# A scan kernel with its skip term and B's turn as TensorE transposes, half of dt*x on VectorE, and a new order of issue

## The chip, the cores and the metric

The kernel runs on one core of a Trainium2 chip. A core has five engines that run their own instruction streams in order: TensorE (PE, matmuls and transposes; its weight loads are shown apart as PEld), VectorE (DVE), ScalarE (ACT), GpSimd (POOL) and SyncE (SP), which here only issues DMAs. They wait for each other by semaphores. Data lies in SBUF; PE writes its results to PSUM.

The metric is the time of one execution on the device in microseconds, from which the median of several runs is taken.

## The reference

The input is 16 images of 64 x 64 tokens with 128 channels. Layer 0 is a two-dimensional recurrent network and stays as it is. Layer 1 is a Mamba block that runs over the 4096 tokens of an image forwards and backwards, with the sum of both added to the input. Cut to what matters:

```python
dbl = xc @ x_w.T
dt, Bm, Cm = jnp.split(dbl, [DT_RANK, DT_RANK + D_STATE], axis=-1)
dt = jax.nn.softplus(dt @ dt_w.T + dt_b)
dA = jnp.exp(dt[..., None] * A)
dBx = dt[..., None] * Bm[:, :, None, :] * xc[..., None]
def step(h, inp):
    dA_t, dBx_t, C_t = inp
    h = dA_t * h + dBx_t
    y = jnp.einsum('bds,bs->bd', h, C_t)
    return (h, y)
...
y = jnp.swapaxes(ys, 0, 1) + xc * D
y = y * jax.nn.silu(z)
return y @ out_w.T
```

There are 256 inner channels (two halves of 128, called h = 0 and 1 below) and 16 states for each channel. All is in float32. D holds 256 factors, one for each channel.

## The kernel before

Layer 0 runs first (`layer0`). Layer 1 (`layer1`) then goes through 256 passes: for each of the 16 images 8 chunks of 512 tokens forwards and the same 8 backwards. A pass has the channels on the 128 partitions and the 512 tokens along the free dimension, once for each half.

In a pass, `conv` (PE) makes the convolved input, `silu` (ScalarE) makes `xc` of it, `xproj` (PE) and `xproj_take` (ScalarE) make `dbl`, which holds dt's low rank, B and C, tokens along the free dimension, in two blocks of 64 partitions for the two halves of the chunk. `dtproj` (PE) and `softplus` (ScalarE) make `dt`. `times` makes `dtx` = dt * xc, for both halves on GpSimd (line 1235). `decay` (ScalarE, line 1254) makes exp(dt * A) for each of the 16 states, and `scan` (VectorE, line 1308) runs the recurrence for each state and half: 32 scans of 512 tokens in a pass.

What goes into the scans besides the decays comes in two ways. For states 0 to 3, `drive` (GpSimd, line 1262) multiplies `dtx` by rows of B that a DMA has spread over all partitions; there the decay lies in a PSUM bank and the product in SBUF. For states 4 to 15, `drive_rows` (PE, line 1288) multiplies the turned `dtx` by a matrix `d` with B's values on diagonals; there the decay lies in SBUF and the product (`hps`) in PSUM. For `d`, `bturn` turns `dbl` on PE so that tokens lie on partitions (line 1182), `bturn_take` copies 12 of its columns to `bt` (ScalarE, line 1193), and `scatter` (SP, line 1271) writes `bt` to the diagonals of a matrix in DRAM, from which `spread` loads it (line 1207). `turn` and `turn_take` turn `dtx` itself.

The results are gathered in one PSUM bank `py` for each half, one half after the other. It begins with `skip` (PE): the matmul of `xc` with `ddiag`, a diagonal matrix of D that is built once, so that D * xc comes out turned, tokens on partitions. Then come `sums` (PE, transposes of `hc` that add up in PSUM, where `hc` is the scans' result times C by GpSimd's `out_of`, line 1331), and for the first four states `turned`, `turned_take` and `weigh`. Both `skip` and `sums` go through the helper `add`, so they share line 1368 and are told apart by their tiles (`py<-ddiag,xc` and `py<-ident,hc`). `finish` takes the half out of `py`; in the backward passes `again` adds the forward result, and `gate`, `back` and `project` lead to the output.

The order of the work on all engines is planned when the program is built: `order_of_issue` lists every operation with its engine, what it must follow and which buffers it takes, and `simulate` runs this list through a model with a cost for each operation (`COST`, `ISSUE`, `LINK`). An engine that is free takes the ready operation with the lowest urgency, and urgencies stand in the table `URGENCY`, one number for each operation in a forward and in a backward pass. The order in which the model begins the operations is the order in which they are issued. `RINGS` gives the number of buffers for each kind of tile, `AHEAD` by how much decays into PSUM banks may leave their order among themselves. The model only sets the order; on the chip each engine waits for what it needs.

Of the kernel before, what the change touches and what calls it, by code (L numbers as in the profile page):

```python
# [8 lines left out]
F32 = mybir.dt.float32  # L9
# [5 lines left out]
P = 128  # L15
# [29 lines left out]
def units_of(order):  # L45

    count = {}
    for x in order:
# [4 lines left out]
        else:  # L53
# [6 lines left out]
    "br": 2, "cr": 6, "bt": 2, "xc": 5, "dt": 4, "dtx": 3, "dtxt": 3, "dbl": 2, "z": 1, "y": 1,  # L60
# [5 lines left out]
    "bturn": 0.5, "bturn_take": 0.23, "xproj": 1.0, "xproj_take": 0.4, "times": 1.2,  # L66
    "turn": 0.47, "turn_take": 0.555, "decay": 0.68, "drive": 2.4, "drive_rows": 1.13,
    "scan": 1.21, "keep": 0.6, "keep_group": 0.57, "out": 2.39, "sums": 0.88, "skip": 0.89,
# [3 lines left out]
    "read_take": 0.56, "read_stats": 0.69, "normal": 3.0, "normalise": 0.75, "spread": 0.6, "rows": 0.81,  # L72
# [10 lines left out]
AHEAD = 3  # L83
# [3 lines left out]
ISSUE = {"b": 0.7, "c": 0.7, "d": 0.51, "k": 0.45, "scatter_d": 0.82, "scatter_k": 1.77}  # L87
# [3 lines left out]
        {(0, 0): 226.07, (0, 1): 225.5, (0, 2): 209.71, (0, 3): 245.13, (1, 0): -224.93, (1, 1): -215.88,  # L91
         (1, 2): -217.49, (1, 3): -219.71},
        {(0, 0): 240.75, (0, 1): 97.67, (0, 2): 239.83, (0, 3): 183.31, (1, 0): -224.93, (1, 1): -236.77,
         (1, 2): -236.93, (1, 3): -239.63},
    ),
    "xproj": (
        {(): -4.49},
        {(): 88.92},
    ),
    "xproj_take": (  # L100
        {(): 12.43},
        {(): -21.38},
    ),
    "rows": (
        {(): -45.24},
        {(): -121.72},
    ),
    "bturn": (
        {(): 244.05},
        {(): -26.43},  # L110
    ),
    "bturn_take": (
        {(): 158.86},
        {(): 159.8},
    ),
    "dtproj": (
        {(0,): -250, (1,): -53.81},
        {(0,): 50.32, (1,): 50.35},
    ),
    "times": (  # L120
        {(0,): -65.05, (1,): -67.57},
        {(0,): 244.56, (1,): -165.67},
    ),
    "turn": (
        {(0,): 249.76, (1,): -134.89},
        {(0,): 229.21, (1,): 221.57},
    ),
    "turn_take": (
        {(0,): 47.45, (1,): 47.51},
        {(0,): 227.25, (1,): 226.2},  # L130
    ),
    "skip": (
        {(0,): 103.25, (1,): 218.48},
        {(0,): 89.87, (1,): 208.37},
    ),
    "spread": (
        {("b", 0): 48.09, ("d", 0): 223.16, ("c", 0): 189.13, ("c", 1): 239.27, ("d", 1): -105.98, ("c",
         2): 8.58, ("c", 3): 235.49, ("b", 1): 201.1, ("d", 2): 56.35, ("c", 4): 230.23, ("c", 5):
         215.44, ("k", 0): 139.69},
        {("b", 0): -14.32, ("d", 0): 47.86, ("c", 0): -35.94, ("c", 1): 138.92, ("d", 1): -107.61, ("c",  # L140
         2): -218.83, ("c", 3): -181.78, ("b", 1): -3.62, ("d", 2): 122.62, ("c", 4): 54.73, ("c", 5):
         240.7, ("k", 0): 139.45},
    ),
    "drive": (
        {(0, 0): -56.91, (1, 0): -57.77, (0, 1): 215.02, (1, 1): 247.85},
        {(0, 0): 171.33, (1, 0): 123.34, (0, 1): 160.79, (1, 1): 118.53},
    ),
    "decay": (
        {(0, 0): 224.88, (4, 0): 226.48, (5, 0): 240.06, (6, 0): 188.37, (7, 0): 250, (1, 0): 113.5, (8,
         0): 247.75, (9, 0): 250, (10, 0): 249.7, (11, 0): 249.33, (2, 0): 123.95, (12, 0): 249.4, (13,  # L150
         0): 176, (14, 0): 177.57, (15, 0): 243.29, (3, 0): 220.69, (4, 1): 238.79, (5, 1): 203.28, (6,
         1): 109.72, (7, 1): 15.19, (0, 1): 44.93, (8, 1): 223.62, (9, 1): 223.58, (10, 1): 225.51, (11,
         1): 223.77, (1, 1): 148.26, (12, 1): 223.35, (13, 1): 66.54, (14, 1): 65.52, (15, 1): 156.31,
         (2, 1): 205.76, (3, 1): 245.25},
        {(0, 0): 114.51, (4, 0): 225.16, (5, 0): 225.14, (6, 0): 226.99, (7, 0): 226.82, (1, 0): 116.2,
         (8, 0): 248.06, (9, 0): -17.84, (10, 0): -182.05, (11, 0): 70.11, (2, 0): 180.88, (12, 0):
         152.1, (13, 0): 166.91, (14, 0): 113.63, (15, 0): 222.06, (3, 0): 31.92, (4, 1): 221.8, (5, 1):
         236.29, (6, 1): 241.63, (7, 1): 222.65, (0, 1): 243.59, (8, 1): 198.45, (9, 1): 228.52, (10, 1):
         31.86, (11, 1): 26.36, (1, 1): 192.12, (12, 1): 244.33, (13, 1): 245.68, (14, 1): 241.41, (15,
         1): 243.62, (2, 1): 241.76, (3, 1): 250},  # L160
    ),
    "scan": (
        {(0, 0): -110.99, (4, 0): -110.09, (5, 0): -105.1, (6, 0): -105.34, (7, 0): -105.61, (1, 0):
         181.32, (8, 0): 19.6, (9, 0): 19.21, (10, 0): -80.71, (11, 0): 7.49, (2, 0): 40.13, (12, 0):
         -108.17, (13, 0): -102.34, (14, 0): -10.85, (15, 0): -108.25, (3, 0): -48.47, (4, 1): -48.83,
         (5, 1): -68.91, (6, 1): -83.82, (7, 1): -96.92, (0, 1): -31.74, (8, 1): -33.58, (9, 1): -38.05,
         (10, 1): -40.96, (11, 1): -50.07, (1, 1): 200.94, (12, 1): -50.19, (13, 1): -87.76, (14, 1):
         -88.26, (15, 1): -91.09, (2, 1): -5.51, (3, 1): -86.39},
        {(0, 0): -109.51, (4, 0): -109.17, (5, 0): -109.22, (6, 0): 181.52, (7, 0): 181.62, (1, 0):
         181.29, (8, 0): 178.29, (9, 0): 89.91, (10, 0): 53.07, (11, 0): 78.05, (2, 0): 236.4, (12, 0):  # L170
         238.58, (13, 0): 235.96, (14, 0): 231.8, (15, 0): 185.76, (3, 0): 215.03, (4, 1): -224.25, (5,
         1): -76.4, (6, 1): -164.06, (7, 1): -249.08, (0, 1): -59.15, (8, 1): 43.77, (9, 1): 17.69, (10,
         1): -44.01, (11, 1): 39.93, (1, 1): 179.06, (12, 1): 225.25, (13, 1): 220.27, (14, 1): 219.29,
         (15, 1): 208.64, (2, 1): 205.77, (3, 1): -93.1},
    ),
    "scatter": (
        {("d", 0): -144.33, ("d", 1): 131.97, ("d", 2): -55.93, ("k", 0): 242},
        {("d", 0): 229.49, ("d", 1): 250, ("d", 2): -140.49, ("k", 0): 202.88},
    ),
    "drive_rows": (  # L180
        {(0, 0): 146.61, (1, 0): 105.78, (2, 0): 191.69, (0, 1): 31.86, (1, 1): 23.35, (2, 1): 216},
        {(0, 0): 117.29, (1, 0): -235.5, (2, 0): -209.5, (0, 1): -218.03, (1, 1): -1.36, (2, 1): 220.27},
    ),
    "keep": (
        {(0, 0): 243.5, (1, 0): 34.18, (2, 0): 129.78, (3, 0): -79.15, (4, 0): 159.92, (5, 0): -249.25,
         (0, 1): 66.3, (1, 1): 176.21, (2, 1): 144.92, (3, 1): -209.94, (4, 1): 140.89, (5, 1): 96.84},
        {(0, 0): -158.59, (1, 0): 220.66, (2, 0): 74.58, (3, 0): -133.66, (4, 0): 174.52, (5, 0): 249.16,
         (0, 1): -179.84, (1, 1): -6.05, (2, 1): -230.81, (3, 1): -175.76, (4, 1): -72.61, (5, 1): 0.64},
    ),
    "out_of": (  # L190
        {(0, 0): 108.7, (1, 0): -34.28, (2, 0): -83.46, (3, 0): 208.24, (4, 0): 161.27, (5, 0): -58.6,
         (0, 1): 206.6, (1, 1): -49.46, (2, 1): -49.85, (3, 1): -249.28, (4, 1): -201.46, (5, 1): 30.29},
        {(0, 0): 70.5, (1, 0): -63.47, (2, 0): -69.72, (3, 0): 41.7, (4, 0): 117.41, (5, 0): 29.34, (0,
         1): -114.11, (1, 1): -106.56, (2, 1): -250, (3, 1): -250, (4, 1): -242, (5, 1): -12.92},
    ),
    "sums": (
        {(0, 0): 211.83, (1, 0): 214.79, (2, 0): 204.06, (3, 0): -118.64, (4, 0): 34.31, (5, 0): -162.93,
         (0, 1): 232.47, (1, 1): 221.1, (2, 1): 203.91, (3, 1): 184.07, (4, 1): -222.45, (5, 1): -216.44},
        {(0, 0): -193.31, (1, 0): -194.97, (2, 0): -209.87, (3, 0): -189.32, (4, 0): -201.67, (5, 0):
         -91.54, (0, 1): 250, (1, 1): 236.49, (2, 1): 104.24, (3, 1): 225.82, (4, 1): 240.77, (5, 1):  # L200
         166.95},
    ),
    "keep_group": (
        {(0, 0): 208.79, (0, 1): -155.94},
        {(0, 0): -223.05, (0, 1): -200.24},
    ),
    "turned": (
        {(0, 0, 0): -242.59, (0, 0, 1): 198.86, (0, 0, 2): -19.69, (0, 0, 3): -164.84, (0, 1, 0): 211.89,
         (0, 1, 1): -221.33, (0, 1, 2): -221.83, (0, 1, 3): -131.66},
        {(0, 0, 0): -224.04, (0, 0, 1): 147.65, (0, 0, 2): -245.55, (0, 0, 3): -163.35, (0, 1, 0):  # L210
         142.63, (0, 1, 1): 126.52, (0, 1, 2): 128.31, (0, 1, 3): 130.7},
    ),
    "turned_take": (
        {(0, 0, 0): 63.6, (0, 0, 1): 44.72, (0, 0, 2): 65.41, (0, 0, 3): 65.32, (0, 1, 0): -184.53, (0,
         1, 1): 128.22, (0, 1, 2): 127.61, (0, 1, 3): 106.49},
        {(0, 0, 0): 55.23, (0, 0, 1): 9.13, (0, 0, 2): 192.65, (0, 0, 3): 192.3, (0, 1, 0): -181.41, (0,
         1, 1): -222.89, (0, 1, 2): 132.46, (0, 1, 3): 131.21},
    ),
    "weigh": (
        {(0, 0): -231.65, (0, 1): -206.75},  # L220
        {(0, 0): -4.68, (0, 1): 4.67},
    ),
# [1276 lines left out]
```

## Time and profile before

| | us |
|---|---|
| median of 3 runs | 12,566.69 (12,562.89 to 12,603.51) |
| profiled execution | 12,569.44 |
| its span, first to last instruction | 12,567.3 |

Busy time over the whole span, layer 0 with it:

| engine | busy us | share |
|---|---|---|
| PE | 12,114.5 | 96% |
| PE weight loads | 9,486.8 | 75% |
| VectorE | 11,138.3 | 89% |
| ScalarE | 9,954.8 | 79% |
| GpSimd | 10,578.2 | 84% |

The granted PE clock is 0.99 of full speed over the span, the DMA engines are busy a little over half of the time. Layer 0 takes the first 1,500 us or so, in which GpSimd has little to do; from there on the profile is even to the end. Matmuls are pipelined and their ends are modelled, so PE's busy time isn't its load. Rows of groups give the engine, the operation, the tiles written and read with their shape, the count, the busy time, the mean duration of one in ns, and the idle time of the engine just before them with what ended it.

### The profile page before, as it was taken

To read this page: it belongs to the slowest core of one execution; us is meant where nothing else is said; L and a number is where in the kernel's file an instruction comes from. 1 tells how busy PE (TensorE), PEld (TensorE's weight loads), DVE (VectorE), ACT (ScalarE), POOL (GpSimd) and SP (SyncE) were. 2 spreads that over 40 slices of the span, in tenths; PEclk is the share of its full clock that TensorE was granted. 3 is DMA by queue.
4 is the path that set the end of the run, shared out by engine and by line. 5 is a ranking of instruction groups with operands and counts; after the bars stand their busy time and mean duration, and the time that the engine had idled before them with its cause. 6 is when DMAs were issued, how large, how long until landed. Compare 5 with 4: busy or idle time off the path is not lost. (4 is left out here: it accounts for less than half of the span.)

```text
span 12567.3 us, 322625 instructions
## 1 busy us (share of the span) xinstructions
PE 12114.5 (96%) x128820; PEld 9486.8 (75%) x128820; DVE 11138.3 (89%) x11409; ACT 9954.8 (79%) x15936; POOL 10578.2 (84%) x4868
## 2 busy tenths in 40 slices
PE   9999999999999999999999999999999999999999
PEld 8656877777777777777777777777777777777777
DVE  7767699998989999999999998999999999999998
ACT  3444588888888888888888888888888888888887
POOL 0111299999999999999999999999999999999998
PEclk9999899999999999999999999999999999999999
DMA  4222255555556555555555555555555555556564
GB/s 156 56 56 56 64 162 160 158 166 158 160 157 166 159 160 158 165 160 158 167 159 162 158 163 161 162 163 158 162 158 163 159 163 161 162 159 165 158 164 140
DMA packets 2320782, 1885.92 MB, mean 150 GB/s; under 512 B 1537696, under 2 KB 1883312, under 8 KB 2319280
## 3 DMA queue, kind: packets, MB, share of 16 engines
q1 hardware_dynamic: 2241328, 1830.04, 52.2%
q10 hardware_dynamic: 77952, 35.24, 1.2%
q8 instruction: 1017, 16.66, 0.5%
q14 instruction: 485, 3.97, 0.1%
HBM read 1698.25 MB, written 164.30 MB: 148 GB/s over the span
## 5 line engine op out<-in xcount | busy, mean ns | idle before, releaser
L1331 POOL TENSOR_TENSOR hc<-hst,cr 128x1024 f32<-128x1024 f32 x3072 | 7384.9, 2431 | 465.0 <-DVE hst L1308 307.3
L1308 DVE TENSOR_TENSOR_SCAN hst<-da,carry,hps 128x512 f32<-128x512 f32 x5376 | 6466.2, 1261 | 535.0 <-issue 219.7
L1254 ACT ACTIVATE da<-dt,A_log_sb 128x512 f32<-128x512 f32 x8192 | 5404.7, 710 | 843.3 <-DVE hst L1308 783.9
L1368 PEld LDWEIGHTS py<-ident,hc 128*128 128x128 f32 x24576 | 2763.6, 142 | 769.0 <-issue 358.3
L1368 PE MATMUL py<-ident,hc 128*128 128x128 f32 x24576 | 3108.0, 275 | 165.7 <-POOL hc L1331 154.5
L1262 POOL TENSOR_TENSOR group<-dtx,br 128x1024 f32<-128x1024 f32 x1024 | 2447.0, 2403 | 134.8 <-PE ptg L1340 85.8
L1308 DVE TENSOR_TENSOR_SCAN group<-da,carry,group 128x512 f32<-128x512 f32 x1792 | 2243.8, 1266 | 118.9 <-ACT da L1254 108.3
L1288 PEld LDWEIGHTS hps<-d,dtxt 32*128 32x128 f32 x49152 | 1526.0, 187 | 621.8 <-issue 280.3
L1125 PE MATMUL pp<-xT,wk 128*128 128x512 f32 x4096 | 1954.8, 599 | 1.7 <-ACT dt L1229 1.2
L1288 PE MATMUL hps<-d,dtxt 32*128 32x128 f32 x49152 | 1810.0, 283 | 139.4 <-DVE hst L1308 117.3
L1348 ACT COPY ht<-ptg 128x512 f32<-128x512 f32 x2048 | 1126.9, 588 | 430.6 <-PE ptg L1340 398.9
L887 POOL TENSOR_TENSOR a_f<-a_f,c 128x16 f32<-128x16 f32 (+35 forms) x254 | 188.6, 743 | 1313.9 <-ACT a_f L879 1250.2
L1340 PE MATMUL ptg<-ident,group 128*128 128x128 f32 x8192 | 1153.0, 278 | 35.4 <-DVE group L1308 18.5
L1340 PEld LDWEIGHTS ptg<-ident,group 128*128 128x128 f32 x8192 | 922.4, 142 | 256.9 <-issue 91.9
L1125 PEld LDWEIGHTS pp<-xT,wk 128*128 128x128 f32 x4096 | 697.5, 190 | 524.9 <-issue 496.1
L1308 DVE TENSOR_TENSOR_SCAN hst<-da,hps 128x512 f32<-128x512 f32 x768 | 874.6, 1199 | 83.8 <-PE hps L1288 46.4
L1235 POOL TENSOR_TENSOR dtx<-dt,xc 128x512 f32<-128x512 f32 x512 | 646.8, 1288 | 61.6 <-DMA d<-d 29.5
L1254 ACT ACT_TABLE_LOAD x527 | 676.1, 1283 | 9.4
L1368 PE MATMUL py<-ddiag,xc 128*128 128x128 f32 x4096 | 580.2, 285 | 13.3 <-ACT y L1415 10.8
L1355 PE MATMUL py<-ht,k 128*32 128x128 f32 x16384 | 559.8, 277 | 2.6 <-ACT ht L1348 1.2
L879 ACT ACTIVATE a_f<-pg_f,b_sb 128x16 f32<-128x16 f32 (+35 forms) x508 | 219.7, 472 | 415.2 <-DMA x<-xl 212.7
L1368 PEld LDWEIGHTS py<-ddiag,xc 128*128 128x128 f32 x4096 | 496.2, 191 | 59.3 <-ACT y L1415 25.4
(113 smaller groups left out, 12431.2 us busy)
## 6 DMA issues: line engine op xcount, KB each, us to landing
cr<-rows SPq DMA_DIRECT2D x1536, 512.0 KB
d<-d SPq DMA_DIRECT2D x768, 448.0 KB
br<-rows SPq DMA_DIRECT2D x512, 512.0 KB
k<-k SPq DMA_DIRECT2D x256, 256.0 KB
yf<-y SPq DMA_DIRECT2D x128, 512.0 KB
yl<-yf SPq DMA_DIRECT2D x128, 512.0 KB
carry<-hst SPq DMA_DIRECT2D x3072, 1.0 KB
xs<-in_x_dram SPq DMA_DIRECT2D x64, 512.0 KB
```

What stands on the lines that cost most here:

```text
L879: nc.scalar.activation(agv.rearrange("p i b -> p (i b)"), pgv, AF.Tanh if g == "c" else AF.Sigmoid, bias=b_sb[:, gi : gi + 1],)
L1125: nc.tensor.matmul(self.ps["conv", h], lhsT=wk[:, k, h * P : (h + 1) * P], rhs=xT[self.b % 2][:, t0 : t0 + T], start=(k == 0), stop=(k == ...
L1235: nc.gpsimd.tensor_mul(self.dtx[h], self.dt[h], self.xc[h])
L1254: nc.scalar.activation(t, self.dt[h], AF.Exp, scale=amat[:, h, s : s + 1])
L1262: nc.gpsimd.tensor_mul(both[:, m : m + 2, :], bc(self.dtx[h], 1, 2), self.brow[q])
L1288: nc.tensor.matmul(part[:, j, :, :], lhsT=self.dtxt[h][rows, j, :], rhs=dg[rows, j + r, :, :], start=True, stop=True, skip_group_check=True,)
L1308: nc.vector.tensor_tensor_scan(t[:, self.rev], self.da.pop((s, h))[:, self.rev], dbx[:, self.rev], 0.0 if self.first else carry[:, self.d, ...
L1331: nc.gpsimd.tensor_mul(self.hc[g, h], self.hst[g, h].rearrange("p t m -> p m t"), self.crow[g])
L1340: nc.tensor.transpose(pt[:, k, :], self.group[g, h][:, t0 : t0 + TB, :].rearrange("p t s -> p (t s)"), ident,)
L1348: nc.scalar.copy(t, self.ps.pop(("turned", g, h, j)))
L1355: nc.tensor.matmul(self.py[h][q * TB : (q + 1) * TB, j * P : (j + 1) * P], lhsT=cd[:, GX * j + q, :], rhs=self.ht[g, h, j][:, q, :], start ...
L1368: nc.tensor.matmul(self.py[h][:, cols], **{"start": False, "stop": False, **how}, skip_group_check=True)
```

## The change

Five things change.

1. `skip` becomes a transpose. ScalarE first makes `xd` = xc * D in a new operation `scaled` (one for each half, ring of two buffers), and PE adds its four 128 x 128 blocks to `py` as transposes against the identity. `ddiag` goes.
2. `bturn` becomes four transposes of 128 rows in place of eight matmuls of 64 x 64. Its result lies on 64 partitions, with the two halves of the chunk side by side, so `bt` has 96 columns on 64 partitions instead of 48 on 128, and each `scatter` of a `d` becomes two DMAs of 64 partitions, six in a pass instead of three.
3. `times` of the second half runs on VectorE, that of the first stays on GpSimd.
4. `dtx` has two buffers instead of three, and `AHEAD` is 0 instead of 3.
5. Some costs of the planner are set anew, and all urgencies are.

```diff
-    "br": 2, "cr": 6, "bt": 2, "xc": 5, "dt": 4, "dtx": 3, "dtxt": 3, "dbl": 2, "z": 1, "y": 1,
+    "br": 2, "cr": 6, "bt": 2, "xc": 5, "xd": 2, "dt": 4, "dtx": 2, "dtxt": 3, "dbl": 2, "z": 1, "y": 1,
...
-    "bturn": 0.5, "bturn_take": 0.23, "xproj": 1.0, "xproj_take": 0.4, "times": 1.2,
-    "turn": 0.47, "turn_take": 0.555, "decay": 0.68, "drive": 2.4, "drive_rows": 1.13,
-    "scan": 1.21, "keep": 0.6, "keep_group": 0.57, "out": 2.39, "sums": 0.88, "skip": 0.89,
+    "bturn": 0.5, "bturn_take": 0.28, "xproj": 1.0, "xproj_take": 0.4, "times": 1.28, "times_dve": 0.62,
+    "turn": 0.47, "turn_take": 0.555, "decay": 0.68, "drive": 2.4, "drive_rows": 1.12,
+    "scan": 1.22, "keep": 0.62, "keep_group": 0.5, "out": 2.43, "sums": 0.92, "skip": 0.45, "scaled": 0.68,
...
-AHEAD = 3
+AHEAD = 0
...
-ISSUE = {"b": 0.7, "c": 0.7, "d": 0.51, "k": 0.45, "scatter_d": 0.82, "scatter_k": 1.77}
+ISSUE = {"b": 0.45, "c": 0.44, "d": 0.46, "k": 0.34, "scatter_d": 1.2, "scatter_k": 0.65}
...
-                put("times", (h,), "POOL", after=[("softplus", i, h), ("silu", i, h)],
-                    takes=[T_["dtx"][h]], uses=[T_["xc"][h], T_["dt"][h]], chain=("times", 0))
+                put("times", (h,), "DVE" if h else "POOL", C_["times_dve"] if h else None, after=[("softplus", i, h), ("silu", i, h)],
+                    takes=[T_["dtx"][h]], uses=[T_["xc"][h], T_["dt"][h]], chain=("times", h))
...
-            put("skip", (h,), "PE", after=[("silu", i, h)], takes=[py[h]], uses=[T_["xc"][h]], chain=("skip", 0))
+            xd = tile_of("xd")
+            put("scaled", (h,), "ACT", after=[("silu", i, h)], takes=[xd], uses=[T_["xc"][h]], chain=("scaled", 0))
+            put("skip", (h,), "PE", after=[get(("scaled", i, h))], takes=[py[h]], uses=[xd, T_["xc"][h]], chain=("skip", 0))
...
-                pt = self.ps["bturn"] = bank(place, f"pbt_{self.nm}", (P, NB, QP))
+                pt = self.ps["bturn"] = bank(place, f"pbt_{self.nm}", (QP, NB, P))
                 strided = self.dbl.rearrange("p (i j) -> p j i", j=NB)
                 for j in range(NB):
-                    for q in range(NQ):
-                        part = slice(q * QP, (q + 1) * QP)
-                        nc.tensor.matmul(
-                            pt[part, j, :],
-                            lhsT=strided[part, j, :],
-                            rhs=ident[part, part],
-                            start=True,
-                            stop=True,
-                            skip_group_check=True,
-                        )
+                    nc.tensor.transpose(pt[:, j, :], strided[:, j, :], ident)
...
-                self.bt = ring(cp, "bt", [P, NB, NS - NX], f"bt_{self.nm}")
-                nc.scalar.copy(self.bt, self.ps.pop("bturn")[:, :, RANK + NX : RANK + NS])
+                self.bt = ring(cp, "bt", [QP, NB, NQ, NS - NX], f"bt_{self.nm}")
+                pt = self.ps.pop("bturn").rearrange("p j (q s) -> p j q s", q=NQ)
+                nc.scalar.copy(self.bt, pt[:, :, :, RANK + NX : RANK + NS])
...
-                nc.gpsimd.tensor_mul(self.dtx[h], self.dt[h], self.xc[h])
+                (nc.vector if h else nc.gpsimd).tensor_mul(self.dtx[h], self.dt[h], self.xc[h])
...
-                    dst = bass.AP(t.tensor, t.offset, [[WD + GX, P], [P, NB], [1, GX]])
-                    nc.sync.dma_start(dst, self.bt[:, :, GX * g : GX * (g + 1)])
+                    for q in range(NQ):
+                        dst = bass.AP(
+                            t.tensor, t.offset + q * QP * (WD + GX), [[WD + GX, QP], [P, NB], [1, GX]]
+                        )
+                        nc.sync.dma_start(dst, self.bt[:, :, q, GX * g : GX * (g + 1)])
...
+            def scaled(self, h):
+                self.xd[h] = ring(cp, "xd", [P, T], f"xd_{self.nm}_{h}")
+                nc.scalar.activation(self.xd[h], self.xc[h], AF.Copy, scale=dvec[:, h, :])
+
             def skip(self, h):
 
                 for j in range(NB):
                     self.add(
                         h,
                         slice(j * P, (j + 1) * P),
-                        lhsT=self.xc[h][:, j * P : (j + 1) * P],
-                        rhs=ddiag[:, h, :],
+                        lhsT=self.xd[h][:, j * P : (j + 1) * P],
+                        rhs=ident,
+                        is_transpose=True,
                     )
```

## The prediction

> **What bounds it now.** I read the page's busy shares first, then a table of stretches, then the groups of instructions between 3000 and 12000 us, then the waits of VectorE, and last two timelines. The chain of waits is of no use here: the page follows it over a few steps and gives every share as 0%.
>
> The groups show 209 passes between 3000 and 12000 us (418 `times` instructions, two a pass). A pass so takes 9000 / 209 = 43.06 us, and the 256 passes of layer 1 take 11,023 us; the rest, some 1,540 us, is layer 0, where only the building of `ddiag` goes. All that follows is per pass, times 256.
>
> The stretch (columns: length, then busy us of PE, weight loads, VectorE, ScalarE, GpSimd):
>
> ```profile
> 3000.00:12000.00 9000.00, 8679.55 (x99538) 6864.47 (x99537) 8229.28 (x7147) 7587.61 (x11748) 8480.52 (x3762) 1.00 0.58 161
> ```
>
> Divided by 209: GpSimd 40.58 us, VectorE 39.37, ScalarE 36.30. PE's 41.5 is modelled and no measure. GpSimd bounds the loop, 2.48 us under the pass; VectorE has 3.69 us of idle time. Who ends VectorE's idle time:
>
> ```profile
> DVE hst L1308 <- issue: 193.4, 457, 1.5
> DVE group L1308 <- ACT da L1254: 124.6, 208, 1.8
> DVE hst L1308 <- PE hps L1288: 120.7, 196, 1.8
> DVE hst L1308 <- POOL hc L1331: 87.1, 142, 1.7
> DVE y L1417 <- PE py L1355: 69.0, 186, 0.7
> DVE hst L1308 <- POOL group L1262: 46.3, 61, 1.6
> ```
>
> No one wait carries it. Waits ended by PE (120.7 + 69.0 here, 23.1 in smaller rows) and by GpSimd (133.4 here, 10.9 for `dtx`) make 357 us, 1.71 a pass. The loop is balanced between three engines, so work taken from one counts only as far as the next allows.
>
> **Skip and B's turn on PE.** From the timeline at 6000 us (start, duration, count):
>
> ```profile
> 6004.83 0.75 PE L1242 MATMUL ptx<-ident,dtx 128*128 128x128 f32 x4
> ...
> 6005.60 1.16 PE L1368 MATMUL py<-ddiag,xc 128*128 128x128 f32 x8
> ...
> 6034.98 0.42 PEld L1340 LDWEIGHTS ptg<-ident,group 128*128 128x128 f32 x4
> 6034.99 0.65 PE L1340 MATMUL ptg<-ident,group 128*128 128x128 f32 x4
> ...
> 6044.65 1.17 PE L1182 MATMUL pbt<-ident,dbl 64*64 64x64 f32 x16
> ```
>
> An fp32 matmul counts as two instructions, a transpose as one: `skip` of one half is 8 now and 4 after. The row nearest to the new skip (four transposes of contiguous data) is ptg, 0.65 us: 1.16 - 0.65 = 0.51 saved, twice a pass, 1.02 us. The Trainium skill ("TensorE: Matmul & The Clock Gate", Terms) calls the transpose mode four times faster for fp32; by that, an estimate, skip would fall to 1.16 / 4 = 0.29 and save 1.74 us a pass. The rows give 1.16 / 0.65 = 1.8 times at this size, and I take them. `bturn`'s 16 instructions become 4 strided transposes, whose row is ptx: 1.17 - 0.75 = 0.42. PE sheds 1.44 us a pass. It doesn't set the end alone, so this pays only through VectorE's waits for PE and the sums' place behind them.
>
> The groups from which the next costs come (count, then busy us and mean ns of one; busy over count is the spacing):
>
> ```profile
> L1331 POOL TENSOR_TENSOR hc<-hst,cr 128x1024 f32<-128x1024 f32 x2508 | 6029.8, 2431 | 375.1 <-DVE hst L1308 242.4 <-DMA cr<-rows 61.0 <-issue 29.1
> ...
> L1254 ACT ACTIVATE da<-dt,A_log_sb 128x512 f32<-128x512 f32 x6695 | 4418.1, 710 | 690.4 <-DVE hst L1308 641.7 <-DVE group L1308 40.4
> ...
> L1348 ACT COPY ht<-ptg 128x512 f32<-128x512 f32 x1672 | 920.4, 588 | 336.3 <-PE ptg L1340 310.1
> ...
> L1235 POOL TENSOR_TENSOR dtx<-dt,xc 128x512 f32<-128x512 f32 x418 | 528.2, 1288 | 27.2 <-ACT dt L1229 18.5
> ```
>
> **ScalarE.** Two `scaled` of 128x512. Lowest by the plain copies of 128x512 (920.4 / 1672 = 0.55 us), highest by the normalise, also SBUF to SBUF (76.4 / 103 = 0.74), and I take the decay's row, which has a scale by partition and no bias (4418.1 / 6695 = 0.66): 1.32 us. No table load: copies stand between exponentials today without one. `bturn_take` moves 96 elements in place of 48, by the slope between the 256- and 512-wide copies (0.367 and 0.588 us) 0.04 more. ScalarE 37.66 us, hidden by its 6.8 us of idle time, because `xc` is ready two passes ahead. If that cover were gone, all 1.36 us would go to the decays behind, 348 us in the run.
>
> **SP.** Three more scatters, 0.50 us each by the median of `d<-bt`: 1.5 us on a queue that mostly waits for scans. Behind them stand `d`, `k`, the C rows and the carries. PE has no wait that ends with `d`'s landing; GpSimd waits for C rows 0.29 us a pass. I count nothing; with every such wait doubled, 75 us.
>
> **dt*x.** GpSimd loses 528.2 / 418 = 1.26 us. VectorE gains an instruction with two SBUF inputs, while its scans and products in layer 1 each have one data operand in PSUM. Layer 0 shows what that means, in the timeline at 802 us:
>
> ```profile
> 802.16 1.17 POOL L887 TENSOR_TENSOR a_f<-a_f,c 128x464 f32<-128x464 f32 x1 [7.40 <-ACT a_f L879]
> ...
> 802.65 1.18 DVE L888 TENSOR_TENSOR a_f<-a_f,c 128x464 f32<-128x464 f32 x1 [1.63 <-ACT a_f L879]
> ...
> 803.93 0.64 DVE L890 TENSOR_TENSOR a_f<-a_f,a_f 128x464 f32<-128x464 f32 x1
> ```
>
> The same shape takes 0.64 us with GpSimd idle (L890) and 1.18 beside it (L888). L888 ends 0.50 us after GpSimd's end (803.83 against 803.33), so it begins to stream only when GpSimd is through. In layer 1 GpSimd is busy 94% of the time, in pieces of 2.42 us (16 a pass) and 1.29. The mean rest of a running piece is (16 x 2.42² + 1.29²) / (2 x (16 x 2.42 + 1.29)) = 1.19 us, times 0.94 = 1.12 us. Then 512 elements at L888's rate after the release, 0.55 us. So `times` of the second half costs VectorE 1.67 us, not 0.69 (0.64 plus 48 elements), and the planner plans 0.62. No row shows the other direction. The Trainium skill ("SBUF — State Buffer", two separate sides) says that the pair of ports is locked for a whole instruction and the other engine blocks fully; by it GpSimd stands 0.55 us. By the row alone GpSimd falls to 39.32, with the rule to 39.87, 141 us in the run apart. I take the rule, since the row fits the lock exactly. What the page doesn't say is who comes first when a next GpSimd instruction is queued as well. Queued behind the waiting product are the scans, for which GpSimd, PE and ScalarE's decays wait.
>
> **Edits with one answer.** One `dtx` buffer fewer: `times` of a pass waits for the same half's drives of the pass before; at most it doubles the 0.22 us a pass in `hst <- POOL group`; I count nothing. `AHEAD` 0, the costs and the urgencies only reorder: what they bring can't be read from this profile, and it is the widest unknown. I bound it by the idle time, at best all 1.71 us that VectorE waits for PE and GpSimd, at worst none of it.
>
> **Sum.** VectorE 39.37 + 1.67 = 41.04 becomes the largest load. Of its idle 3.69 us, the waits for PE (less loaded by 1.44) and GpSimd (by 0.71) go in part: all gone gives 41.04 + 1.98 = 43.02 (10 us less in the run), half gone 43.88 (+210 us). I take three quarters, 1.28: 41.04 + 2.41 = 43.45, +0.39 x 256 = +100 us, nearer to the low end because both engines in front have new slack, and not at it because the issue order was laid out for a VectorE that doesn't wait. The profiled execution took 12,569.4 us (span 12,567.3); the median 12,566.7 is the same within 3 us. Forecast **12,667 us**, own range 12,605 to 12,780.
>
> **Rivals.**
> 1. *Faster: GpSimd goes on to decide.* VectorE's wait falls into its 3.69 us of idle time, and the pass follows GpSimd: 39.87 + 2.48 = 42.35, -0.71 x 256 = -182, **12,385 us**. For it: VectorE waits as often as GpSimd is busy, and GpSimd is largest today. Against: idle VectorE time is mostly there to wait for inputs, and the product doesn't bring them sooner. It decides as soon as over 1.3 us of the added 1.67 lie in old gaps. Were there no lock at all, 41.80 and 12,244.
> 2. *Slower by much: the product loses the race.* If GpSimd's queued instruction takes the ports first, the product waits one more piece, 2.42 us: 43.45 + 2.42 = 45.87, +719, **13,286 us**. For: GpSimd runs its pieces without gap. Against: a request that already waits should be served, and layer 0, with one piece at a time, can't tell.
> 3. *Nothing measurable:* relief and wait cancel, **12,567 us**, as the low end of the sum already has it.
>
> **Chances.** Forecast case 0.46, rival 1 0.33, rival 2 0.10, rival 3 0.11. A change under 0.3% (38 us) can't be told from none here. So faster 0.33, same 0.11, slower 0.56. The range for 8 in 10 goes from rival 1's number to well above the forecast case and leaves out most of rival 2 and rival 1's lower part: 12,400 to 12,940. For the forecast case alone it is 12,605 to 12,780.
>
> **What would show it.** Right: `dtx` on VectorE with a mean near 1.7 us and a spread from 0.7 to 3; some GpSimd instructions 0.5 us longer beside it; skip as 4 instructions in 0.65 us; VectorE's share up to 94 or 95%, GpSimd's down to 92%; two ACT instructions of 0.7 us a pass without new table loads; the granted clock still 1.00. Wrong: `dtx` at 0.7 us (no lock, then rival 1 or better), `dtx` over 3 us (rival 2), or waits of VectorE for `da` or `hps` that grow, which would put the loss on the order of issue and not on the ports.

## The result, and the profile after

| | before | after |
|---|---|---|
| median, us | 12,577.49 (12,562.89 to 12,603.51, 4 runs) | 13,051.31 (13,008.00 to 13,067.97, 4 runs) |
| profiled execution, its span | 12,569.44, 12,567.3 | 13,008.0, 13,006.2 |

The changed kernel is slower: ratio 1.0369, 95% interval 1.0336 to 1.0402. That is 474 us by the medians, and 439 us between the two profiled executions, from which all that follows is read.

The stretch from 3000 to 12000 us of the kernel after (columns as in the prediction: busy us of PE, weight loads, VectorE, ScalarE, GpSimd, then the granted clock, the DMA share and GB/s):

```profile
3000.00:12000.00 9000.00, 8165.16 (x91695) 6378.92 (x91693) 8238.95 (x7086) 7525.26 (x11717) 7992.38 (x3420) 0.98 0.55 155
```

It holds 201 passes, so a pass takes 9000 / 201 = 44.78 us, 1.72 more than before; times 256 that is 440 us, the whole difference of the profiled executions. Per pass (measured busy time, and idle time as the rest of the pass):

| us per pass | before | predicted | after |
|---|---|---|---|
| VectorE busy | 39.37 | 41.04 | 40.99 |
| GpSimd busy | 40.58 | 39.87 | 39.76 |
| ScalarE busy | 36.30 | 37.66 | 37.44 |
| VectorE idle | 3.69 | 2.41 | 3.79 |
| GpSimd idle | 2.48 | 3.58 | 5.02 |

The loads are as predicted within 0.3 us. The loss lies in idle time: VectorE's didn't shrink, and GpSimd's doubled. Groups of instructions of the kernel after in that stretch (count, busy us and mean ns of one, then idle time just before them and what ended it):

```profile
L1382 ACT ACTIVATE xd<-xc,D_sb 128x512 f32<-128x512 f32 x402 | 289.2, 719 | 60.5 <-PE py L1365 54.9
...
L1229 DVE TENSOR_TENSOR dtx<-dt,xc 128x512 f32<-128x512 f32 x201 | 385.9, 1920 | 0.0
...
L1328 POOL TENSOR_TENSOR hc<-hst,cr 128x1024 f32<-128x1024 f32 x2415 | 5827.6, 2437 | 564.3 <-DVE hst L1305 201.6 <-issue 132.0 <-PE ptg L1337 120.9
...
L1256 POOL TENSOR_TENSOR group<-dtx,br 128x1024 f32<-128x1024 f32 x804 | 1968.7, 2454 | 387.9 <-DMA carry<-group 172.6 <-PE ptg L1337 95.2 <-DVE group L1305 26.0
```

The last row is the one to stop at: GpSimd's products for states 0 to 3 (`drive`, four in a pass) now wait 387.9 us in this stretch, 172.6 of them by name for the DMA of `keep_group`, which copies the last column of a `group` tile into `carry` for the next chunk. The same group before:

```profile
L1262 POOL TENSOR_TENSOR group<-dtx,br 128x1024 f32<-128x1024 f32 x836 | 1998.0, 2404 | 117.3 <-PE ptg L1340 74.7 <-DMA carry<-group 20.9 <-DVE hst L1308 15.4
```

The two new transposes, in the timeline of the kernel after (start, duration, count):

```profile
6009.77 0.65 PE L1182 MATMUL pbt<-ident,dbl 128*64 128x128 f32 x4
...
6012.45 0.66 PE L1365 MATMUL py<-ident,xd 128*128 128x128 f32 x4
```

And who ends VectorE's waits, after (us in total, times, longest):

```profile
DVE hst L1305 <- POOL hc L1328: 240.2, 274, 3.5
...
DVE hst L1305 <- PE hps L1285: 140.6, 168, 2.7
...
DVE group L1305 <- ACT da L1248: 56.7, 56, 2.9
...
DVE y L1419 <- PE py L1352: 3.2, 13, 0.3
```

VectorE's wait for GpSimd's outputs rose from 87.1 to 240.2 us; its waits for the sums on PE fell from 69.0 to 3.2, and those for the decays from 124.6 to 56.7. Some waits went as hoped, and one took their place: VectorE stands for a GpSimd that itself came late.

### The profile page after: what moved, and what is told of

Same layout as the page of the kernel before. It is cut to its first block, busy times and chain, and to the rows that moved or that the text cites. A ratio compares the mean times of both kernels' runs of the same rounds, so it can differ in the third digit from the quotient of the medians.

```text
span 13006.2 us, 313375 instructions
## 1 busy us (share of the span) xinstructions
PE 11893.2 (91%) x123700; PEld 9220.6 (71%) x123700; DVE 11524.1 (89%) x11663; ACT 10233.8 (79%) x16448; POOL 10362.6 (80%) x4612
## 5 line engine op out<-in xcount | busy, mean ns | idle before, releaser
L1365 PE MATMUL py<-ident,hc 128*128 128x128 f32 x24576 | 3208.4, 279 | 350.7 <-POOL hc L1328 349.7
L1365 PEld LDWEIGHTS py<-ident,hc 128*128 128x128 f32 x24576 | 2817.0, 144 | 806.9 <-POOL hc L1328 522.2
L1256 POOL TENSOR_TENSOR group<-dtx,br 128x1024 f32<-128x1024 f32 x1024 | 2508.5, 2456 | 481.6 <-DMA carry<-group 236.5
L1127 PE MATMUL pp<-xT,wk 128*128 128x512 f32 x4096 | 1898.5, 600 | 0.5 <-DVE xl L913 0.5
L1337 PE MATMUL ptg<-ident,group 128*128 128x128 f32 x8192 | 1208.0, 280 | 113.6 <-DVE group L1305 45.6
L1127 PEld LDWEIGHTS pp<-xT,wk 128*128 128x128 f32 x4096 | 739.0, 193 | 711.3 <-issue 684.9
L1213 PE MATMUL pv<-dbl,dt_wT 128*128 128x256 f32 x2048 | 519.9, 383 | 0.0
L1352 PEld LDWEIGHTS py<-ht,k 128*32 128x32 f32 x16384 | 410.6, 110 | 133.1 <-issue 75.8
L1229 DVE TENSOR_TENSOR dtx<-dt,xc 128x512 f32<-128x512 f32 x256 | 467.5, 1826 | 3.8 <-ACT dt L1223 3.8
```

What stands on the lines that cost most here:

```text
L1127: nc.tensor.matmul(self.ps["conv", h], lhsT=wk[:, k, h * P : (h + 1) * P], rhs=xT[self.b % 2][:, t0 : t0 + T], start=(k == 0), stop=(k == ...
L1213: nc.tensor.matmul(pv[:, q * TQ : (q + 1) * TQ], lhsT=dt_wT[:, q, h * P : (h + 1) * P], rhs=self.dbl, start=True, stop=True,)
L1229: (nc.vector if h else nc.gpsimd).tensor_mul(self.dtx[h], self.dt[h], self.xc[h])
L1256: nc.gpsimd.tensor_mul(both[:, m : m + 2, :], bc(self.dtx[h], 1, 2), self.brow[q])
L1337: nc.tensor.transpose(pt[:, k, :], self.group[g, h][:, t0 : t0 + TB, :].rearrange("p t s -> p (t s)"), ident,)
L1352: nc.tensor.matmul(self.py[h][q * TB : (q + 1) * TB, j * P : (j + 1) * P], lhsT=cd[:, GX * j + q, :], rhs=self.ht[g, h, j][:, q, :], start ...
```

## The experiments

Every ratio is to the kernel before, run beside it on the same chip, with its 95% interval. The kernel before took 12,636.5 us beside the first four kernels below, 12,636.7 beside those named `g` and 12,566.9 beside those named `h`, so ratios are to be compared, not times. The lock in the expectations is the wait of VectorE's product for a running GpSimd instruction.

### One part of the change put back, in the new order

`e1_times_back`:

```diff
-                (nc.vector if h else nc.gpsimd).tensor_mul(self.dtx[h], self.dt[h], self.xc[h])
+                nc.gpsimd.tensor_mul(self.dtx[h], self.dt[h], self.xc[h])
```

> The changed kernel with dt*x of both halves on GpSimd again, in the places of its order where they stand now; nothing else differs. Lock theory (VectorE's product waits for GpSimd's piece, 1.92 us a time, and GpSimd's pieces stand up to 0.55 us beside it): VectorE falls from 41.0 to 39.1 us a pass, GpSimd rises from 39.8 to 40.5, the pass goes back to about 43.1 and the time to 12,500 to 12,700. Order theory (the new urgencies, AHEAD 0 and two dtx buffers leave the engines waiting in turn whatever runs where): 12,950 to 13,100. Scatter theory (six scatters on SP's queue make the carries and the C rows late): as by the order theory, 12,950 to 13,100.

Measured: 13,129.85 us, ratio 1.0394 [1.0376, 1.0411]. Taking the product off VectorE gains nothing here, so neither the product nor its lock can be what holds the changed kernel.

`e4_bturn_back`, B's turn again as 64 x 64 matmuls, with three scatters in place of six:

```diff
-                    nc.tensor.transpose(pt[:, j, :], strided[:, j, :], ident)
+                    for q in range(NQ):
+                        part = slice(q * QP, (q + 1) * QP)
+                        nc.tensor.matmul(pt[part, j, :], lhsT=strided[part, j, :], rhs=ident[part, part], ...)
...
-                    for q in range(NQ):
-                        nc.sync.dma_start(dst, self.bt[:, :, q, GX * g : GX * (g + 1)])
+                    nc.sync.dma_start(dst, self.bt[:, :, GX * g : GX * (g + 1)])
```

> The changed kernel with bturn as eight 64x64 matmuls again and three scatters of 128 partitions in a pass, order of issue kept. Lock theory and order theory: within 60 us of the changed kernel's 13,051, since PE's 0.5 us more a pass have 4 us of slack. Scatter theory: SP issues 3 DMAs less (some 2.4 us a pass), GpSimd's waits for the carries of the group (0.86 us a pass) go, and the time falls by 150 to 400 us, to 12,650 to 12,900.

Measured: 13,070.73 us, ratio 1.0339 [1.0320, 1.0358], 0.3% under the changed kernel's 1.0369, and the two intervals overlap. The three added scatters and the new turn together cost little or nothing; the two weren't parted. Taking three issues a pass off SyncE's queue is thus worth little by itself.

`e5_skip_back`, the skip again by `ddiag`, without the two scaled copies:

```diff
-                self.xd[h] = ring(cp, "xd", [P, T], f"xd_{self.nm}_{h}")
-                nc.scalar.activation(self.xd[h], self.xc[h], AF.Copy, scale=dvec[:, h, :])
...
-                        lhsT=self.xd[h][:, j * P : (j + 1) * P],
-                        rhs=ident,
-                        is_transpose=True,
+                        lhsT=self.xc[h][:, j * P : (j + 1) * P],
+                        rhs=ddiag[:, h, :],
```

> The changed kernel with skip as a matmul of xc with the diagonal of D again, and no scaled copies on ScalarE; order of issue kept. Lock, order and scatter theories: within 80 us of 13,051. If ScalarE's 1.44 us of scaled copies a pass delay the decays, the time falls by up to 300; if PE's relief by skip is what holds the time down, it rises by up to 250.

Measured: 13,192.28 us, ratio 1.0441 [1.0425, 1.0458]. The skip as transposes gains 0.7% in this order. So no single part, put back, takes the loss away.

### One part alone, in the order of before

`b1_times_only`, the kernel before with

```diff
-                nc.gpsimd.tensor_mul(self.dtx[h], self.dt[h], self.xc[h])
+                (nc.vector if h else nc.gpsimd).tensor_mul(self.dtx[h], self.dt[h], self.xc[h])
```

> The kernel before with dt*x of the second half on VectorE, in the place of its order where it stands now; nothing else differs. Lock theory: VectorE gains about 1.7 to 1.9 us a pass and GpSimd loses 1.26 and stands 0.55, the time rises by 250 to 450 to 12,830 to 13,030. Order theory and scatter theory: the product alone costs little and GpSimd's relief is worth as much, 12,450 to 12,700.

Measured: 12,785.94 us, ratio 1.0122 [1.0105, 1.0139]. The product on VectorE costs 1.2% by itself, less than the lock theory had it and more than the others.

`g2_skip_only`, the kernel before with the skip of the change (the inverse of the diff of `e5_skip_back`); room for `xd` comes from half of the buffer of `in_wT`, which is loaded in two parts. `g3_skip_times` adds the line of `b1_times_only` to it.

> The kernel before, in its own order, with skip as transposes and the scaled copies put behind the copy of the turned dtx (first half) and behind the first copy of the turned group (second half); half of in_wT's room is given to the new buffers. If the transposes are worth what they were in the new order (skip back cost 0.7%): ratio 0.990 to 0.997. If ScalarE's 1.44 us a pass eat the gain: 0.998 to 1.008.

> g2_skip_only with dt*x of the second half on VectorE as well. With the order of before kept, the cost of the product is that of b1_times_only: ratio 0.010 to 0.014 above g2_skip_only. If PE's relief gives VectorE room for the product: under 0.006 above it.

Measured: `g2_skip_only` 12,595.20 us, 0.9964 [0.9951, 0.9977]; `g3_skip_times` 12,771.38 us, 1.0103 [1.0081, 1.0125]. The skip gains 0.4%, the product takes 1.4% on top of it. By these parts, the change should be 1% slower, not 3.7%. (B's turn wasn't tried in the old order.)

### The order alone

`g4_order_only` is the kernel after with its order of issue and its two `dtx` buffers, but with all work as before: the edits of `e1_times_back`, `e4_bturn_back` and `e5_skip_back` together. `g5_order_br3` gives it a third buffer for the B rows. Of all waits of SyncE's queue, the one for these buffers had grown most from the kernel before (first line) to the one after (second; us in total, times, longest):

```profile
SPq L1213 <- POOL group L1262: 254.3, 214, 2.6
...
SPq L1207 <- POOL group L1256: 532.5, 332, 5.6
```

> The order of issue of the changed kernel with the work of the kernel before: skip by the diagonal of D, bturn as matmuls, dt*x of both halves on GpSimd, three scatters; two dtx buffers stay. Order theory: all of the loss is here, ratio to before 1.037 to 1.050. If the loss needs the new work in the new order (the tables were made for it), the ratio is below 1.025.

> As g4_order_only, with three buffers for the rows of B in place of two, while the order is still the one planned for two. Queue theory (in the new order SP stands at the load of B's rows until GpSimd frees a buffer, 2.6 us a pass against 1.2 before, and the C rows and carries behind it come late): the ratio falls by 0.010 to 0.025 against g4_order_only. If the loss comes from how the engines wait for each other and not from SP's queue: within 0.004 of g4_order_only.

Measured: `g4_order_only` 13,006.36 us, 1.0287 [1.0267, 1.0308]; `g5_order_br3` 12,986.91 us, 1.0265 [1.0242, 1.0289]. **The order with its two `dtx` buffers, and the old work, loses 2.9%**. That lies between the two expectations: most of the loss is here, not all. The fewer `dtx` buffers show no wait of their own: all idle time before GpSimd's `times` is for `dt`.

```profile
L1240 POOL TENSOR_TENSOR dtx<-dt,xc 128x512 f32<-128x512 f32 x402 | 515.8, 1288 | 52.8 <-ACT dt L1234 52.8
```

The queue's long stand at the B rows is only the place at which it waits, hardly a cause: a third buffer takes 0.2%, within the noise.

### What in the order: a small copy that lands late

I laid the trace of the kernel after beside its order of issue, pass by pass. In the passes of the backward direction GpSimd keeps step until the `drive` that opens the second half. There GpSimd stands 2.87 us per pass (before: not at all). It needs a `group` buffer, and that is free only when PE has turned it (`turned`) and `keep_group`, a DMA of 2 KB on SyncE's queue, has read its last column. One such place in the timeline of the kernel after (start, duration; SPq is SyncE's queue; in brackets the idle time before and its releaser):

```profile
6283.25 3.60 DVE L1305 TENSOR_TENSOR_SCAN group<-da,carry,group 128x512 f32<-128x512 f32 x3
...
6284.51 2.69 SPq L1317 DMA_DIRECT2D carry<-hst  x1
...
6287.29 0.54 SPq L1207 DMA_DIRECT2D cr<-rows  x1
...
6287.93 0.49 SPq L1321 DMA_DIRECT2D carry<-group  x1
6288.51 0.54 SPq L1207 DMA_DIRECT2D cr<-rows  x1
...
6293.93 2.39 POOL L1256 TENSOR_TENSOR group<-dtx,br 128x1024 f32<-128x1024 f32 x1 [3.85 <-DMA carry<-group]
```

The last scan of the group ends at 6286.85. The queue has a carry and a load of C rows (512 KB) ahead, and reaches the small DMA at 6287.93, 1.08 us later. GpSimd starts 5.51 us after that issue's end (6288.42), having stood 3.85 us. So 7 us go from the scan to the next product.

The trace also has the single packets that the DMA engines moved. The 128 packets of the small copy, 16 bytes each, begin at 6291.92 us, 3.5 us after the issue, and the last begins at 6293.28; from 6289.00 on the engines move packets of 4 KB, which by the order of the queue are C rows. GpSimd starts 0.65 us after the last small packet began. In 73 of the 97 such passes of the stretch these packets can be told from others. Counted from the issue's end, the first of them begins after 3.2 us and GpSimd starts after 5.0 us, both in the median. In all 73 it starts 0.6 to 1.3 us after the last small packet began, also in the 29 where the view names another releaser than this DMA. So the stand of 2.87 us is this copy's, and not only the part with its name. The same copy of the first half always has a carry of 1 KB ahead of it in these passes, not a load of 512 KB, and there its packets begin 0.66 us after the issue.

The test takes the DMA away: ScalarE copies the column, at the same place of the order. That also takes two issues a pass off SyncE's queue, but three fewer gained only 0.3% (`e4_bturn_back`). The edit was made to four kernels: the one after (`h1_keep_on_act`), the one before as a control (`h0_before_keep_on_act`), the old work in the new order (`h4_order_keep`, on `g4_order_only`) and the skip alone (`h3_skip_keep`, on `g2_skip_only`).

```diff
             def keep_group(self, g, h):
 
-                nc.sync.dma_start(
+                nc.scalar.copy(
                     carry[:, self.d, h, g * GX : (g + 1) * GX], self.group[g, h][:, self.last, :]
                 )
```

> The kernel after, with the copy of a state group's last column into carry made by ScalarE instead of by a DMA on SyncE's queue, at the same place of the order. Theory of the late carry: in the backward passes GpSimd stands 2.87 us per pass before the second half's first product, because the group buffer is freed only by that small DMA, which SyncE issues late (behind a carry or a recall of 512 KB) and which lands 3 to 5 us after; with a copy on ScalarE the buffer is free some 0.5 us after the scan, the stand goes, and with it most of the backward passes' loss: between 150 and 300 us less than the kernel after, a ratio to before of 1.012 to 1.026. Rival, the order is too tight in general (each wait that goes is replaced by the next: scans for GpSimd's outputs, GpSimd for the hst ring): less than 60 us, ratio 1.032 to 1.039.

> The kernel before with the same edit, as the control. Theory of the late carry: before's order leaves GpSimd over 5 us between the carry's landing and the next use of the buffer in the backward passes and some 1 us of idle per pass in the forward ones, so little is to be had: ratio 0.990 to 1.000. Rival, the carries' DMA costs every order the same: as much as in the run of the kernel after with this edit (150 us or more, ratio below 0.988).

> The order of the kernel after with the work of the kernel before, and the carry's copy on ScalarE. Late carry: the order alone cost 1.0287, its second-half gap on GpSimd was 1.47 us backward and 0.70 forward; it goes, ratio 1.010 to 1.020. Order too tight in general: 1.024 to 1.029.

> The kernel before with the skip as transposes and x scaled by D on ScalarE, and the carry's copy on ScalarE. If the two gains add: 0.9964 times the control's ratio, 0.987 to 0.997. If ScalarE becomes late by the copies (0.2 to 0.3 us each, two or four per pass): above 1.000.

| | median us | ratio [95%] | same kernel with the DMA |
|---|---|---|---|
| `h1_keep_on_act` | 12,690.64 | 1.0089 [1.0070, 1.0108] | 1.0369 |
| `h0_before_keep_on_act` | 12,536.93 | 0.9976 [0.9967, 0.9986] | 1 |
| `h4_order_keep` | 12,804.90 | 1.0188 [1.0170, 1.0206] | 1.0287 |
| `h3_skip_keep` | 12,492.55 | 0.9939 [0.9924, 0.9953] | 0.9964 |

The one edit takes 2.8% from the changed kernel, more than expected, and 0.24% from the one before (both in percent of the time before). The stretch and the two groups of `h1_keep_on_act`:

```profile
3000.00:12000.00 9000.00, 8363.07 (x94439) 6539.24 (x94440) 8483.90 (x7295) 7775.25 (x12468) 8226.63 (x3519) 0.98 0.56 159
```

```profile
L1256 POOL TENSOR_TENSOR group<-dtx,br 128x1024 f32<-128x1024 f32 x828 | 2032.2, 2460 | 132.6 <-PE ptg L1337 132.6
...
L1321 ACT COPY carry<-group 128x4 f32<-128x4 f32 x414 | 77.5, 187 | 50.7 <-DVE group L1305 50.3 <-POOL hc L1328 0.3
```

Its waits of VectorE:

```profile
DVE hst L1305 <- PE hps L1285: 89.9, 146, 2.7
...
DVE hst L1305 <- POOL hc L1328: 58.1, 146, 3.1
```

The wait for `carry<-group` is gone, the copy takes 0.187 us, and VectorE's wait for GpSimd's outputs is down from 240.2 to 58.1 us. GpSimd's idle time before `drive` fell from 387.9 to 132.6 us, 1.29 us a pass, nearly the whole gain of 1.30 us a pass: VectorE's shorter wait is the same gain seen from the other side. With 207 passes a pass takes 43.48 us; VectorE is busy 40.98 and idle 2.49.

The passes of the two directions, timed in the traces from the first `drive` of one direction to that of the next and divided by eight (images 2 to 15), say where the edit works:

| us per pass | forward | backward |
|---|---|---|
| before | 42.75 | 43.48 |
| after | 43.80 | 45.66 |
| `h1_keep_on_act` | 44.08 | 42.97 |
| `b1_times_only` | 44.09 | 43.62 |

The copy gives back all that the backward passes had lost, and more; there GpSimd's stand falls from 2.87 to 0.25 us. The forward passes gain nothing.

`h4_order_keep` limits the finding: with the old work the new order still loses 1.9%. With the new work it loses 0.9%, about what the skip and the product cost together in the old order (1.0%). So once the copy is out of the way, the order seems as good for the new work as the old order was, by the sum of the parts and not by a run; it is poor for the old work, for which it wasn't laid out. Of the 2.9% that the order costs the old work, the late copy explains 1.0 point, and the rest is open.

`h3_skip_keep` is faster than both kernels: 0.6% under the one before. The two gains add (0.9964 x 0.9976 = 0.9940).

**Left open.** That the small copy is late because a load of 512 KB is ahead of it on the queue is read from the packets; no run moved that load. Nor was it settled what the new order loses in the forward passes, where GpSimd's stand before that `drive` is 0.85 us against 1.05 before, and its first outputs wait 1.9 us against 0.4. The product on VectorE makes them as long in the old order (44.09 us), but with the product back on GpSimd they stay long in the new one (43.74 us in `e1_times_back`).

## Why the prediction was wrong

The direction was right, and the time outside the range: 12,667 predicted, at most 12,940, and 13,051 measured.

**Right: the loads.** Skip 0.66 us against 0.65 predicted; B's turn 0.65 against 0.75. The scaled copies have a spacing of 0.72 us against the decay's 0.66. VectorE 40.99 against 41.04, GpSimd 39.76 against 39.87, ScalarE 37.44 against 37.66. VectorE's closeness is in part luck: its product takes 0.25 us more than forecast, and its other work 0.30 us less than before. To go by the row (1.8 times) and not by the four times that the prediction also names was right: 1.16 to 0.66 is 1.8.

**Right: the lock, and in both directions, but not its mean.** The instructions of the two products and of `drive`, after (duration ns, lowest, median, highest):

```profile
L1256 POOL TENSOR_TENSOR group<-dtx,br x804: 2359/2399/2894, 3008.0 to 11987.0; 128x1024 f32<-128x1024 f32 x161
L1229 POOL TENSOR_TENSOR dtx<-dt,xc x201: 1269/1284/1780, 3001.5 to 11954.8; 128x512 f32<-128x512 f32 x101
L1229 DVE TENSOR_TENSOR dtx<-dt,xc x201: 855/1194/7531, 3004.1 to 11957.7; 128x512 f32<-128x512 f32 x101
```

Wherever a GpSimd piece ends while the product stands, the product ends 0.55 us after the last such piece (median), as the prediction had it from layer 0. The slowest GpSimd pieces take 0.5 us more than their median, which is the other direction, as the prediction took it. The mean is 1.92 us (predicted 1.67), but it hangs on where the order puts the product. In the kernel after, it begins beside a running GpSimd piece all 201 times; in the old order (`b1_times_only`) it finds GpSimd idle 108 times of 205, and its mean is 1.05:

```profile
L1235 DVE TENSOR_TENSOR dtx<-dt,xc 128x512 f32<-128x512 f32 x205 | 214.5, 1046 | 0.0
```

The prediction's mean rest of a piece takes the product to come at a random time, and it doesn't. In the old order, 1.05 us a pass are 268 us in the run, and 149 us showed in the time.

**Half right: rival 2.** The product does lose the race, up to three pieces long (7.5 us): behind two or three pieces 21 times of 201, and all 20 that take over 5 us are in forward passes. The prediction had it as all or nothing, at 2.42 us each; it is rare, and lies within the mean of 1.92.

**Right, as far as tried: scatters at nothing** (`e4_bturn_back`, 0.3% by the medians, with B's turn put back as well), though the median time of one issue rose from 0.50 to 0.615 us.

**Wrong: the order.** The step that failed is this: "`AHEAD` 0, the costs and the urgencies only reorder: what they bring can't be read from this profile, and it is the widest unknown. I bound it by the idle time, at best all 1.71 us that VectorE waits for PE and GpSimd, at worst none of it." The worst end was missing: an order can also make new idle time. It cost 2.9% with the old work. In the changed kernel, 2.8 of the 3.7% hang on one buffer: GpSimd stands 2.87 us in each backward pass until a small DMA has read it, where the prediction had no term for a wait that the old order didn't have. With it fell "three quarters" of the waits that were to go: VectorE's idle time went to 3.79 us and not to 2.41. The sign that the prediction named for a loss by the order came only in part: VectorE's waits for `hps` grew (120.7 to 140.6 us), those for `da` fell (124.6 to 56.7), and the wait that grew most was for GpSimd's outputs. The profile before had the thread in hand, `group<-dtx,br` waiting 20.9 us for `carry<-group`: a buffer freed by a DMA that had to land, with the slack given only by the order that was about to be replaced.

With the late copy removed, the sum comes out: 43.48 us a pass against the forecast's 43.45, VectorE's idle time 2.49 against 2.41, and 12,690.64 us against 12,667. That is closer than the argument deserves, since the copy on ScalarE also gains 30 us for the kernel before, and since the mean hides forward passes 1.33 us longer than before and backward ones 0.51 us shorter.

**Wrong, with little weight:** the granted clock didn't stay at 1.00 but fell to 0.98. It is 0.98 in `h1_keep_on_act` too, which is rid of three quarters of the loss, so it isn't the cause of these.

**Rival 1** (GpSimd decides, faster) fell: GpSimd lost load and gained idle time, 2.48 to 5.02 us. The price of the prediction's `dtx` buffer fewer wasn't tried by itself; it is part of `g4_order_only`, where `times` has no wait for a buffer.

## What to carry to other kernels

An edit that lays the order of issue anew has a bad end as well as a good one, and neither shows in the loads: before pricing it, list the buffers that are freed by a DMA, and ask how much slack the old order left them. A small copy that frees a buffer on the path belongs on an engine with idle time, if one has it; here 0.19 us of ScalarE took the place of some 5 us of landing. And to find what an order costs, run it with the old work: one run told what putting parts back one by one couldn't. It tells it for the old work only: the same edit took 2.8% from the new work in this order and 1.0% from the old.

## What the runs showed of the hardware

A VectorE product of 128x512 with two SBUF inputs waits for a running GpSimd piece and ends 0.55 us after it; beside an idle GpSimd it took 0.67 us (`b1_times_only`). In the kernel after it waited for one piece 180 times of 201, but 20 times for three that followed without a gap, up to 7.5 us.

The engine that waited for a DMA of 2 KB started 5.0 us after its issue (median of 73) where a load of 512 KB was ahead of it on the queue; the packets began 3.2 us after the issue there, and 0.66 us after it behind a DMA of 1 KB.

Four fp32 transposes of 128 x 128 took 0.66 us on contiguous input (`py<-ident,xd`) and 0.75 on strided input (`ptx`); `pbt`, strided too, took 0.65, but its blocks are 128 x 64.
